# A three-stage decoder layer in float32: SyncE's transfers in program order, loads placed by hand, and the feed-forward's end moved into the next half

## The chip, the cores and the metric

The kernel runs on one core of a Trainium2 chip. The metric is the device time of one execution in microseconds (us). TensorE (PE), VectorE (DVE), ScalarE (ACT) and GpSimd (POOL) compute; SyncE (SP) issues nearly all transfers between device memory and the on-chip buffer.

## The reference, cut to what matters

Three residual stages follow one another, each behind a layer norm without learned factors. `x` has 4 batches of 1024 tokens of width 512, `ctx` 4 batches of 1024 tokens of width 384; there are 16 heads of width 32, and everything is float32.

```
def _layernorm(x, axis=-1, eps=1e-05): ...
# stage 1: gated self-attention
aperture = sigmoid(x @ Wa + ba); expression = sigmoid(x @ We + be)
inner = heads(x @ Wi); outer = heads(x @ Wo)
attn = softmax(einsum('bhqd,bhkd->bhqk', inner, outer) / sqrt(dh), -1)
attn = attn * aperture[..., :, None] * expression[..., None, :]
attn = attn / (attn.sum(-1, keepdims=True) + 1e-08)
converged = einsum('bhqk,bhkd->bhqd', attn, heads(x @ Wv))
...   # a fixed rotation and gains per head
return combined @ Wout
# stage 2: cross-attention to ctx
q = heads(query @ Wq + bq); k = heads(ctx @ Wk + bk); v = heads(ctx @ Wv + bv)
attn = softmax(clip(q k^T * scale))
return (attn v) @ Wo + bo
# stage 3: feed-forward, 512 -> 64 units, each with its own 16-wide layer
s = x @ Win + bin_
h = relu(s[..., None] * W1 + b1)            # (b, t, 64, 16)
g = einsum('btmh,mh->btm', h, W2) + b2
return g @ Wout + bout
# the layer
x = x + stage1(_layernorm(x)); x = x + stage2(_layernorm(x), ctx); x = x + stage3(_layernorm(x))
```

## The kernel before

**Units, halves, steps.** The function that runs is `moderate_path` (`general_path` is entered only if a flag, computed at the end, asks for it). Its work is a list `order` of eight units: units 0 to 3 are the self-attention of batches 0 to 3 (phase 0), units 4 to 7 the cross-attention of the same batches together with the feed-forward (phase 1). A unit has two halves of 512 query tokens, written here as 4.0 (unit 4, half 0) and 4.1. The attention of a half is 32 steps: four groups of four heads, and for each group eight tiles of 128 keys.

**A step.** It issues eight score products (L547, in the trace 16 instructions), two exps on ScalarE (L552, each 128x1024, six buffers `e`), running sums of the exps on VectorE (`es`, L558 and L560; in phase 0 also `eg`, L568), and then the `av` products of the step before (L574). Where the sums of the third and fourth head are taken by TensorE (`shared`: phase 0 and unit 7), products `sm` (L582) follow. After the last step of a group come `normalize` (copies L591, L593), one step later `add_up` (products over the partitions L604, a copy L605, then on SyncE the sums to device memory, L610 and L615, and back in another layout, `cs`, L612, L616, L620), two steps later `divide` (VectorE L628 to L643, the reciprocals to device memory, L644, and back spread over partitions, `recb`, L648), and two steps later `multiply` (VectorE L654), after which the group's quarter of `q` holds the attention's result.

**Work beside the steps.** `run(attention(u, hf), beside(u, hf))` distributes a list of items over the 32 steps of a half, by weights. The items are projections of the next unit (`pre`: `load` of weights, `x`, `ctx`, `ln` layer norm, `xT` the load of the rows just stored as blocks, `tr` their transposes on VectorE, L302, and products `k`, `q`, `v` through `columns`, L87, each evacuated by ScalarE or VectorE, L264 to L268), and the end of the half before (`post`). `post` consists of `load` (output weights `wo` and four residual tiles, L694), `o` (output projection by L87 and the addition of the residual L711), `ln` (L287 with stores of the rows, L291), `xT` (L296), `b` (the output bias, GpSimd L748), `tr`, `s` (the product with Win, L758), `h` (17 items `hidden`: a relu on ScalarE, L773, into one of two buffers `hid`, and an accumulation `g` on VectorE, L777 and L779) and `out` (two items `outputs`: products L790 into two banks, additions L796, stores L798). `weave(a, b)` spreads list `a` evenly over list `b`; `pause(n)` is an empty weight.

**Buffers.** Banks for all products of the items come from one pool of two (`bank`). Weights have three buffers (`w`, loaded at L92 or L128), residual tiles four, inputs (`inT`) two, transposed blocks (`tok`, p1) one.

**Order.** TensorE, VectorE, ScalarE and GpSimd execute in the order in which the program issues. SyncE is not in that list (L57): a scheduler puts its transfers in an order of its own. [...]

**The tail.** After the last step the remaining `add_up`, `divide` and `multiply` of the last group are issued (the list `soon`), and then the whole `post` of half 7.1, with its transposes made by TensorE (L309).

Of the kernel before, what the change touches and what calls it, by code (L numbers as in the profile page):

```python
# [16 lines left out]
P = 128  # L17
# [25 lines left out]
@with_exitstack  # L43
def decoder_kernel(ctx: ExitStack, tc: tile.TileContext, a: dict, out: bass.AP):

    nc = tc.nc
    keep = ctx.enter_context(tc.tile_pool(name="keep", bufs=1))
    flag = keep.tile([1, 1], I32, name="flag")
    E = mybir.EngineType
    with tc.manual_schedule(engines={E.PE, E.DVE, E.Activation, E.Pool}):  # L57
        moderate_path(tc, a, out, flag)
    again = nc.values_load(flag[0:1, 0:1], min_val=0, max_val=1, skip_runtime_bounds_check_because="0 or 1")
    with tc.If(again > 0):  # L60
        general_path(tc, a, out)


def moderate_path(tc: tile.TileContext, a: dict, out: bass.AP, flag: bass.AP):
    nc = tc.nc
    x = a["x"]
    with ExitStack() as st:
# [268 lines left out]
        def pre(u):  # L336
# [145 lines left out]
            def values(kt):  # L482
# [5 lines left out]
                def part(cs):  # L488
                    def f():
                        if cs[0] == 0:  # L490
                            if kt == 0:
                                me["wv"] = load_w(f"v{ph}")
                                me["v"] = p2.tile([P, NT, H, DH], F32, tag="v", name="v")
                            me["pv"] = bank()
                        for c in cs:
                            columns(
                                me["pv"], me[kind, hf, "t"](c, t), me["wv"][:, c, :],
                                start=(c == 0), stop=(c == n - 1),
                            )
                        if cs[-1] == n - 1:  # L500
                            pvh = me["pv"].rearrange("p (h d) -> p h d", d=DH)
                            if ph == 0:
                                ex = me["sw"][:, kt, :, 1].unsqueeze(2).to_broadcast([P, H, DH])
                                nc.vector.tensor_tensor(me["v"][:, kt], pvh, ex, ALU.mult)
                            else:
                                evacuate(me["v"][:, kt], pvh)
# [23 lines left out]
        def attention(u, hf):  # L530
# [5 lines left out]

            shared = ph == 0 or u + 1 == len(order)

            def scores(g, kt):
# [61 lines left out]
            def add_up(g, i, both, added):  # L601
# [11 lines left out]
                else:  # L613
# [5 lines left out]
                    for k in range(sums):  # L619
                        nc.sync.dma_start(  # L620
                            c[64:, k, :, :], s2[k].rearrange("(p h) (q e) -> (h q) p e", h=2, e=INNER)
                        )
                after(2, lambda: divide(g, i, both, c))

            def divide(g, i, both, c):
# [21 lines left out]
                for j in range(HG):  # L647
                    nc.sync.dma_start(  # L648
                        all_[j * DH : (j + 1) * DH, :], rec_d[i % 4][j : j + 1, :].to_broadcast([DH, HALF])
                    )  # L650
                after(2, lambda: multiply(g, both, all_))

# [25 lines left out]
        def post(u, hf):  # L678
# [6 lines left out]
            def load(t):  # L685
                def f():
                    if t == 0:
                        me["wo"] = load_w(f"o{ph}")
                    r = res[t] = p4.tile([P, D], F32, tag="res", name="res")
                    tt = 4 * hf + t  # L690
                    if ph == 0:
                        nc.sync.dma_start(r, x[b][tt * P : (tt + 1) * P, :])
                    else:
                        nc.sync.dma_start(r, x1b_d[b][tt])  # L694
                return f

            def project(t):
                def part(cs):
                    def f():
# [3 lines left out]
                        for c in cs:  # L703
                            columns(
                                res["po"], me["q", hf][:, c, ts(t, P)], me["wo"][:, c, :],
                                start=(c == 0), stop=(c == NC - 1),
# [79 lines left out]
            def outputs(t):  # L786
# [14 lines left out]
            loads = [[(0, load(t)) for t in range(4)]]  # L801
            r = {
                "load": loads,
                "o": [project(t) for t in range(4)],
# [44 lines left out]
        def one(f):  # L849
            return [[(0, f)]]  # L850

        def beside(u, hf):

            last = post(u, 0) if hf else post(u - 1, 1) if u else None
            if u + 1 == n:
                out = last["load"] + pause(16) + last["o"] + weave(last["ln"], pause(4)) + last["xT"] + pause(4)
                out += last["tr"] + weave(last["b"], pause(4)) + last["s"] + weave(last["h"], pause(12))
                return out + pause(2) + last["out"]
            p = pres[u + 1]
            x, ln, xT, tr, k, q, v = (p[i] for i in ("x", "ln", "xT", "tr", "k", "q", "v"))  # L860
            next_ = pres[u + 2] if u + 2 < B else None
            if u + 1 < B:
                if hf == 0:
                    if last:
                        out = x[1] + last["load"] + k[0][0:1] + p["g"][0] + k[0][1:] + p["gt"][0]
                        out += weave(ln[1], last["o"]) + xT[1] + weave(last["ln"], v[0][0:2])
                    else:
                        out = one(rotations) + one(fold_bv) + x[1] + k[0][0:1] + [rotate(c) for c in range(NC)]
                        out += p["g"][0] + k[0][1:2] + [[(4, fold_bv)]] + weave(ln[1], k[0][2:]) + p["gt"][0]
                        out += xT[1] + v[0][0:2]  # L870
                    return out + tr[1] + v[0][2:3] + p["g"][1] + v[0][3:] + p["gt"][1]
                if not next_:
                    return k[1] + last["load"] + v[1] + last["o"] + weave(last["ln"], q[0][0:2]) + q[0][2:] + q[1]
                out = next_["x"][0] + k[1][0:2] + last["load"] + weave(next_["ln"][0], k[1][2:] + v[1]) + last["o"]
                out += weave(last["ln"], q[0][0:2]) + q[0][2:] + next_["xT"][0] + q[1][0:3] + next_["tr"][0] + q[1][3:]
# [5 lines left out]
            if hf == 0:  # L881
                out = p["ctx"][0] + p["ctx"][1] + last["load"]
                if "s" not in last:
                    return out + k[0] + v[0] + last["o"] + weave(last["ln"], k[1][0:2]) + k[1][2:] + v[1][0:2]
                out += k[0][0:3] + v[0][0:1] + last["o"] + weave(last["ln"], v[0][1:3]) + last["xT"] + v[0][3:]
                out += last["b"][0:2] + k[1][0:1] + last["tr"] + k[0][3:] + last["b"][2:] + last["s"]
                return out + weave(last["h"], k[1][1:] + v[1][0:1]) + v[1][1:2] + last["out"]
            out = xT[0] + last["load"] + v[1][2:] + tr[0] + xT[1] + q[0][0:2] + last["o"][0:2] + tr[1] + last["o"][2:]
            out += weave(last["ln"], q[0][2:3])
            if "s" not in last:  # L890
                return out + q[0][3:] + q[1]
            out += last["xT"] + last["b"][0:2] + q[0][3:] + last["tr"] + q[1][0:1] + last["b"][2:] + last["s"]
# [5 lines left out]
        first += p["k"][1] + one(lambda: pres[1]["load"]("k")) + pres[1]["x"][0] + p["g"][1]  # L898
        first += weave(pres[1]["ln"][0], p["q"][1]) + pres[1]["xT"][0] + one(load_wout) + p["gt"][1]
# [668 lines left out]
```

## Time and profile before

| | us |
|---|---|
| median of 3 runs | 2324.78 |
| lowest and highest | 2324.44, 2326.49 |
| the profiled execution, its own time | 2323.08 |
| its span in the profile | 2321.1 |
| TensorE busy | 2214.6 (95%) |
| VectorE busy | 1556.0 (67%) |
| ScalarE busy | 1237.3 (53%) |
| before half 0.0 | 0 to 114.9 |
| phase 0 (0.0 to 3.1) | 114.9 to 1219.8 |
| 4.0, 4.1 | 121.8, 134.6 |
| 5.0, 5.1 | 135.0, 137.1 |
| 6.0, 6.1 | 135.1, 137.4 |
| 7.0, 7.1 to its last step | 117.0, 118.3 |
| tail | 65 |

A half is counted from its first exp (L552) to the first exp of the next. The mean granted TensorE clock is 0.982 of full speed. The share of busy time is a mean over stages that differ: a row of matmuls counts as busy also while its instructions follow one another slowly, so that lengths of halves, and of steps in them, are the better measure of where time goes. Lines of the profile name engine, line, operation, output and input; "idle before <- releaser" tells for how long the engine stood still and what ended that.

### The profile page before, as it was taken

What the parts mean: (1) busy time and instruction counts of PE and PEld (TensorE: products, weight loads), DVE (VectorE), ACT (ScalarE), POOL (GpSimd) and SP (SyncE); (2) the same over time, 40 slices, a digit from 0 to 9 for tenths busy, and PEclk for the clock granted to TensorE, in tenths of its full rate; (3) what the DMA queues carried; (4) which work ended last, traced back from release to release, by engine and by line L of the source; (5) the groups of instructions that cost most, each with busy time, mean ns of one, the idle gap of its engine ahead of it and who ended that gap; (6) DMA issues with size and microseconds to landing.
All of it is one profiled execution on the core that took longest, in us unless ns stands there. A gap on an engine that the chain in (4) does not pass through costs nothing.

```text
span 2321.1 us, 52855 instructions
## 1 busy us (share of the span) xinstructions
PE 2214.6 (95%) x22610; PEld 556.3 (24%) x22610; DVE 1556.0 (67%) x2478; ACT 1237.3 (53%) x1485; POOL 136.9 (6%) x146
## 2 busy tenths in 40 slices
PE   6999999999999999999999999998999989999984
PEld 2322222222222222222222222222222212222211
DVE  4468666786758866666775758776776757645554
ACT  0055445554455544555556555656465645657561
POOL 3000020000000000000000001010010101000000
PEclk9999999999999999999999999999999999999997
DMA  4422032041311312112222212231222332102020
GB/s 132 129 94 67 26 114 71 23 131 37 128 45 35 100 48 84 44 44 85 62 80 57 90 55 74 74 83 62 60 61 75 79 101 61 65 25 70 25 71 25
DMA packets 153862, 162.01 MB, mean 70 GB/s; under 512 B 46624, under 2 KB 92320, under 8 KB 152464
## 3 DMA queue, kind: packets, MB, share of 16 engines
q1 hardware_dynamic: 150160, 157.48, 22.6%
q8 instruction: 179, 2.93, 0.6%
q0 software_dynamic: 2144, 0.98, 0.3%
q14 instruction: 67, 0.55, 0.1%
q10 hardware_dynamic: 1312, 0.07, 0.1%
HBM read 115.68 MB, written 42.76 MB: 68 GB/s over the span
## 4 chain that ended last, share of the span: by engine, by line
PE 82%; DVE 5%; DMA 5%; ACT 4%; issue 3%; SPq 1%; DVEq 0%; ACTq 0%
PE f L87 33%; PE s L547 22%; PE av L574 18%; PE sm L582 5%; PE sm L604 3%; ACT e L552 2%; DVE es L560 2%; DMA rec_d<-rec 2%; ACT hid L773 1%; PE f L790 1%; DMA w<-in_attn_Wo 1%; DVE g L779 1%; DMA recb<-rec_d 1%; DMA rows_d<-r 1%; SPq L648 0%
## 5 line engine op out<-in xcount | busy, mean ns | idle before, releaser
L552 ACT ACTIVATE e<-s 128x1024 f32<-128x1024 f32 x1024 | 994.3, 1021 | 767.3 <-PE s L547 579.3
L560 DVE TENSOR_TENSOR es<-es,e 128x1024 f32<-128x1024 f32 x528 | 637.7, 1233 | 265.1 <-ACT e L552 263.9
L547 PE MATMUL s<-q,k 32*64 32x512 f32 x8192 | 635.0, 616 | 24.8 <-ACT e L552 22.6
L574 PE MATMUL av<-e,v 128*32 128x512 f32 x4096 | 553.7, 606 | 0.0
L87 PE MATMUL f<-xT,w 128*32 128x512 f32 x2816 | 335.7, 601 | 16.7 <-DVE xT L302 15.9
L568 DVE SCALAR_TENSOR_TENSOR eg<-e,sw,eg 128x512 f32<-128x512 f32 x448 | 318.4, 746 | 2.3
L87 PE MATMUL f<-w,q 128*32 128x512 f32 x2048 | 245.6, 597 | 11.3 <-DVE q L654 11.3
L547 PEld LDWEIGHTS s<-q,k 32*64 32x64 f32 x8192 | 138.5, 130 | 490.4 <-ACT e L552 288.3
L558 DVE TENSOR_TENSOR es<-e 128x1024 f32<-128x1024 f32 x88 | 110.3, 1276 | 205.2 <-ACT e L552 184.0
L574 PEld LDWEIGHTS av<-e,v 128*32 128x32 f32 x4096 | 88.4, 108 | 406.9 <-issue 401.4
L87 PEld LDWEIGHTS f<-xT,w 128*32 128x32 f32 x2816 | 93.2, 111 | 233.1 <-issue 205.3
L582 PE MATMUL sm<-e,sw 128*2 128x512 f32 x1024 | 133.3, 592 | 0.0
L773 ACT ACTIVATE hid<-sT,units 128x256 f32<-128x256 f32 x128 | 73.4, 600 | 72.3 <-DVE sT L268 40.7
L87 PEld LDWEIGHTS f<-w,q 128*32 128x32 f32 x2048 | 67.1, 111 | 167.5 <-issue 151.1
L719 POOL TENSOR_TENSOR r<-res,bo_bc 128x512 f32<-128x512 f32 x32 | 40.9, 1277 | 1111.5 <-DVE res L711 1056.5
L87 PE MATMUL f<-w,xT 128*32 128x512 f32 x896 | 104.6, 592 | 0.6 <-DVE q L268 0.6
L87 PE MATMUL f<-ctxT,w 128*32 128x512 f32 x768 | 92.7, 592 | 0.0
L87 PE MATMUL f<-w,ctxT 128*32 128x512 f32 x768 | 91.9, 593 | 0.0
L779 DVE SCALAR_TENSOR_TENSOR g<-hid,units,g 128x256 f32<-128x256 f32 x120 | 58.0, 483 | 34.4 <-ACT hid L773 25.2
L604 PE MATMUL sm<-es,ones 128*1 128x512 f32 x352 | 68.5, 621 | 0.7 <-ACT both L593 0.7
L654 DVE TENSOR_TENSOR q<-both,recb 128x512 f32<-128x512 f32 x64 | 45.0, 703 | 34.5 <-DMA recb<-rec_d 34.1
L287 DVE TENSOR_SCALAR r<-res,fmv,yi 128x512 f32<-128x512 f32 x60 | 37.1, 635 | 38.4 <-DMA rows_d<-r 37.8
(240 smaller groups left out, 1068.2 us busy)
## 6 DMA issues: line engine op xcount, KB each, us to landing
recb<-rec_d SPq DMA_DIRECT2D x256, 64.0 KB
xT<-rows_d SPq DMA_DIRECT2D x60, 256.0 KB
rows_d<-r SPq DMA_DIRECT2D x60, 256.0 KB
w<-in_xattn_Wo SPq DMA_DIRECT2D x9, 1024.0 KB
xin<-in_x SPq DMA_DIRECT2D x8, 1024.0 KB
res<-in_x SPq DMA_DIRECT2D x32, 256.0 KB
w<-wout_d SPq DMA_DIRECT2D x8, 1024.0 KB
x1b_d<-r SPq DMA_DIRECT2D x32, 256.0 KB
```

What stands on the lines that cost most here:

```text
L87: nc.tensor.matmul(to[r], lhsT=lhsT[:, j, :] if len(lhsT.shape) == 3 else lhsT[:, r], rhs=rhs, **flags)
L547: nc.tensor.matmul(s[m : m + 64, j, :], lhsT=k[r, g, kt * P + m : kt * P + m + 64], rhs=q[r, g, :], start=True, stop=True,)
L552: nc.scalar.activation(e, s, AF.Exp, scale=SCALE)
L558: nc.vector.tensor_tensor(me["es"][i], me["e", 0][i], es[i], ALU.add)
L560: nc.vector.tensor_tensor(me["es"][i], me["es"][i], es[i], ALU.add)
L568: nc.vector.scalar_tensor_tensor(eg, es[0][:, h, :], gate(kt), eg, ALU.mult, ALU.add)
L574: nc.tensor.matmul(av[r, :], lhsT=me["v"][:, kt, HG * g + h, :], rhs=es[h // 2][:, h % 2, :], start=(kt == 0), stop=(kt == NT - 1),)
L582: nc.tensor.matmul(sm[j * DH : j * DH + sums, :], lhsT=me["sw"][:, t, HG * g + 2 + h, :] if ph == 0 else ones, rhs=me["e", t][1][:, h, :], ...
L604: nc.tensor.matmul(sm[j * DH : j * DH + 1, :], lhsT=ones, rhs=e, start=True, stop=True)
L654: nc.vector.tensor_tensor(me["q", hf][:, g, :], both[:, 0, :], all_, ALU.mult)
L773: nc.scalar.activation(hid, res["s"], AF.Relu, bias=units[:, 1, h : h + 1], scale=units[:, 0, h : h + 1])
L779: nc.vector.scalar_tensor_tensor(res["g"], res["hid"], units[:, 2, h - 1 : h], res["g"], ALU.mult, ALU.add)
```

## The change

- **SyncE in program order.** L57 puts SyncE into the list of engines whose order is the program's. Each load of weights is an item of its own in the lists: `ahead(u, "k" | "q" | "v")` for a coming unit's, `wo` for the output weights, apart from the residual's `load`.
- **A half's feed-forward ends in the next half.** The items `h` and `out` of the half whose `s` has just been made are kept in `held`. In the next half, `end(...)` weaves the 17 hidden items with the first products (`k[0] + v[0][0:1]` in half 0, `v[1][2:] + q[0][0:2]` in half 1) and puts the outputs after them; the residual loads of the following `post` come after that.
- **Transposes earlier.** `xT[0]`, two value items and `tr[0]` go to the end of half 0; before, `xT[0]` and `tr[0]` stood at the head of half 1.
- **Unit 7.** Sums, `divide` and `multiply` are `apart` three steps instead of two. Half 7.1 makes six of the hidden items of (7, 0).
- **The tail.** The other eleven hidden items of (7, 0), the last half but one, are issued between the last group's `add_up`, `divide` and `multiply` (six and five), its `out` after them, ahead of the output projection of 7.1. The residual of 7.1 goes to a buffer of `inT`.

```
-    with tc.manual_schedule(engines={E.PE, E.DVE, E.Activation, E.Pool}):
+    with tc.manual_schedule(engines={E.PE, E.DVE, E.Activation, E.Pool, E.SP}):
...
+            apart = 2 if u + 1 < len(order) else 3
...
-                after(2, lambda: divide(g, i, both, c))
+                after(apart, lambda: divide(g, i, both, c))
...
-                after(2, lambda: multiply(g, both, all_))
+                after(apart, lambda: multiply(g, both, all_))
...
-                    if t == 0:
-                        me["wo"] = load_w(f"o{ph}")
-                    r = res[t] = p4.tile([P, D], F32, tag="res", name="res")
+                    if not last:
+                        r = res[t] = p4.tile([P, D], F32, tag="res", name="res")
+                    else:
+                        if t == 0:
+                            res["all"] = p2.tile([P, 4, D], F32, tag="inT", name="res")
+                        r = res[t] = res["all"][:, t, :]
...
+            def fetch():
+                me["wo", hf] = load_w(f"o{ph}")
...
+        held = []
+        def ahead(u, what):
+            return one(lambda: pres[u]["load"](what))
...
             last = post(u, 0) if hf else post(u - 1, 1) if u else None
+            end = lambda items: weave(held[0]["h"], items) + held.pop()["out"] if held else items
             if u + 1 == n:
-                out = last["load"] + pause(16) + last["o"] + weave(last["ln"], pause(4)) + last["xT"] + pause(4)
-                out += last["tr"] + weave(last["b"], pause(4)) + last["s"] + weave(last["h"], pause(12))
-                return out + pause(2) + last["out"]
+                out = last["wo"] + end(pause(14)) + last["load"] + pause(2) + last["o"] + weave(last["ln"], pause(8))
+                out += last["xT"] + pause(10) + last["tr"] + weave(last["b"], pause(4)) + last["s"]
+                if hf == 0:
+                    out += pause(5)
+                else:
+                    out += weave(last["h"][0:6], pause(6))
+                    last["h"] = last["h"][6:]
+                held.append(last)
+                return out
...
             if hf == 0:
-                out = p["ctx"][0] + p["ctx"][1] + last["load"]
-                if "s" not in last:
-                    return out + k[0] + v[0] + last["o"] + weave(last["ln"], k[1][0:2]) + k[1][2:] + v[1][0:2]
-                out += k[0][0:3] + v[0][0:1] + last["o"] + weave(last["ln"], v[0][1:3]) + last["xT"] + v[0][3:]
-                out += last["b"][0:2] + k[1][0:1] + last["tr"] + k[0][3:] + last["b"][2:] + last["s"]
-                return out + weave(last["h"], k[1][1:] + v[1][0:1]) + v[1][1:2] + last["out"]
-            out = xT[0] + last["load"] + v[1][2:] + tr[0] + xT[1] + q[0][0:2] + last["o"][0:2] + tr[1] + last["o"][2:]
-            out += weave(last["ln"], q[0][2:3])
-            if "s" not in last:
-                return out + q[0][3:] + q[1]
-            out += last["xT"] + last["b"][0:2] + q[0][3:] + last["tr"] + q[1][0:1] + last["b"][2:] + last["s"]
-            return out + weave(last["h"], q[1][1:]) + last["out"]
+                out = ahead(u + 1, "v") + last["wo"] + p["ctx"][1] + end(k[0] + v[0][0:1]) + last["load"] + v[0][1:2]
+                out += last["o"] + weave(last["ln"], v[0][2:])
+                if "s" in last:
+                    out += last["xT"] + weave(last["b"], k[1][0:2]) + last["tr"] + k[1][2:3] + last["s"] + k[1][3:]
+                    held.append(last)
+                else:
+                    out += k[1]
+                return out + xT[0] + v[1][0:2] + tr[0]
+            out = ahead(u + 1, "q") + last["wo"] + end(v[1][2:] + q[0][0:2]) + xT[1]
+            out += (ahead(u + 2, "k") if u + 2 < n else []) + last["load"] + q[0][2:3] + last["o"] + tr[1]
+            out += weave(last["ln"], q[0][3:] + q[1][0:1])
+            out += pres[u + 2]["ctx"][0] if u + 2 < n else []
+            if "s" in last:
+                out += last["xT"] + weave(last["b"], q[1][1:3]) + last["tr"] + q[1][3:] + last["s"]
+                held.append(last)
+                return out
+            return out + q[1][1:]
...
-        first = p["x"][0] + p["ln"][0] + p["tr"][0] + p["k"][0] + p["x"][1] + one(negate) + p["g"][0]
+        first = ahead(0, "k") + p["x"][1] + ahead(0, "q") + ahead(0, "v")
+        first += p["x"][0] + p["ln"][0] + p["tr"][0] + p["k"][0] + one(negate) + p["g"][0]
...
-        while soon:
-            soon.pop(0)[-1]()
         crossing.clear()
-        run([lambda: None], sum(post(n - 1, 1).values(), []))
+        tail, before = post(n - 1, 1), held.pop()
+        parts = lambda *names: sum((sum(tail[k], []) for k in names), [])
+        hidden = sum(before["h"], [])
+        run([lambda: None], [parts("wo", "load")])
+        soon.pop(0)[-1]()
+        run([lambda: None], [hidden[0:6]])
+        soon.pop(0)[-1]()
+        run([lambda: None], [hidden[6:]])
+        soon.pop(0)[-1]()
+        run([lambda: None], [sum(before["out"], []), parts("o", "ln", "xT", "b", "tr", "s", "h", "out")])
```

The lists of phase 0 keep their products and get `wo` and `ahead` items: in half 0 `ahead(u + 1, "v")` before the first `k` product, in half 1 `ahead(u + 1, "q")` and `ahead(u + 2, "k")` before `o`.

More of the change, by code (lines that the diff above doesn't have):

```diff
@@ L491, in f @@
                             if kt == 0:
-                                me["wv"] = load_w(f"v{ph}")
+                                if "wv" not in me:
+                                    fetch("v")
                                 me["v"] = p2.tile([P, NT, H, DH], F32, tag="v", name="v")
@@ L704, in f @@
                             columns(
-                                res["po"], me["q", hf][:, c, ts(t, P)], me["wo"][:, c, :],
+                                res["po"], me["q", hf][:, c, ts(t, P)], me["wo", hf][:, c, :],
                                 start=(c == 0), stop=(c == NC - 1),
@@ L802, in post @@
             r = {
+                "wo": [[(0, fetch)]],
                 "load": loads,
@@ L864, in beside @@
                     if last:
-                        out = x[1] + last["load"] + k[0][0:1] + p["g"][0] + k[0][1:] + p["gt"][0]
+                        out = x[1] + last["wo"] + last["load"] + ahead(u + 1, "v") + k[0][0:1] + p["g"][0] + k[0][1:] + p["gt"][0]
                         out += weave(ln[1], last["o"]) + xT[1] + weave(last["ln"], v[0][0:2])
@@ L868, in beside @@
                         out = one(rotations) + one(fold_bv) + x[1] + k[0][0:1] + [rotate(c) for c in range(NC)]
-                        out += p["g"][0] + k[0][1:2] + [[(4, fold_bv)]] + weave(ln[1], k[0][2:]) + p["gt"][0]
-                        out += xT[1] + v[0][0:2]
+                        out += ahead(u + 1, "v") + p["g"][0] + k[0][1:2] + [[(4, fold_bv)]] + weave(ln[1], k[0][2:])
+                        out += p["gt"][0] + xT[1] + v[0][0:2]
                     return out + tr[1] + v[0][2:3] + p["g"][1] + v[0][3:] + p["gt"][1]
                 if not next_:
-                    return k[1] + last["load"] + v[1] + last["o"] + weave(last["ln"], q[0][0:2]) + q[0][2:] + q[1]
-                out = next_["x"][0] + k[1][0:2] + last["load"] + weave(next_["ln"][0], k[1][2:] + v[1]) + last["o"]
+                    out = k[1] + ahead(u + 1, "q") + last["wo"] + last["load"] + v[1] + ahead(u + 2, "k") + last["o"]
+                    return out + weave(last["ln"], q[0][0:2]) + q[0][2:] + pres[u + 2]["ctx"][0] + q[1]
+                out = next_["x"][0] + k[1][0:2] + last["wo"] + last["load"] + weave(next_["ln"][0], k[1][2:] + v[1])
+                out += ahead(u + 1, "q") + ahead(u + 2, "k") + last["o"]
                 out += weave(last["ln"], q[0][0:2]) + q[0][2:] + next_["xT"][0] + q[1][0:3] + next_["tr"][0] + q[1][3:]
@@ L897, in moderate_path @@
+        first += p["x"][0] + p["ln"][0] + p["tr"][0] + p["k"][0] + one(negate) + p["g"][0]
         first += weave(p["ln"][1], p["q"][0]) + p["gt"][0] + p["xT"][1] + p["v"][0][0:3] + p["tr"][1] + p["v"][0][3:]
-        first += p["k"][1] + one(lambda: pres[1]["load"]("k")) + pres[1]["x"][0] + p["g"][1]
+        first += p["k"][1] + pres[1]["x"][0] + ahead(1, "k") + p["g"][1]
         first += weave(pres[1]["ln"][0], p["q"][1]) + pres[1]["xT"][0] + one(load_wout) + p["gt"][1]
```

## The prediction

> **What bounds the kernel now.** I read the busy times, the slices, the table by stretches (one per half), then the waits, the timelines round the longest ones, and the tail. The span is 2321.1 us.
>
> ```profile
> PE 2214.6 (95%) x22610; PEld 556.3 (24%) x22610; DVE 1556.0 (67%) x2478; ACT 1237.3 (53%) x1485; POOL 136.9 (6%) x146
> ...
> PE   6999999999999999999999999998999989999984
> ```
>
> TensorE is the bound nearly throughout, and idle for 106.5 us: by the stretches 19 before the first half, 5 in phase 0, 37 in 4.0 to 6.1 (unit 4, half 0, to unit 6, half 1), 45 in unit 7 and the tail. Since a busy matmul row includes matmuls that crawl, I measured each step from its first exp to the next step's first exp and took off its matmuls at their undisturbed durations (per instruction 0.065 us scores, 0.110 av, 0.114 L87, 0.107 sums). A step with 16 L87 instructions has 16x0.065+8x0.110+16x0.114 = 3.74 us; undisturbed ones take 3.71 to 3.76. What a step takes beyond that is its excess. Phase 0 has 0 to 4 us a half; 4.0 has 3.6, then 4.1 to 7.1 have 15.5, 12.7, 18.4, 12.6, 18.6, 21.4, 19.7. So only phase 1 and the ends have anything to win. From the stretches (length, PE busy, ...), first 4.0, then 5.1:
>
> ```profile
> 1219.80:1341.60 121.80, 121.68 (x1272) 29.92 (x1270) 80.53 (x103) 74.71 (x88) 5.12 (x4) 1.00 0.24 76
> ...
> 1611.20:1748.20 137.00, 128.18 (x1276) 30.55 (x1274) 96.24 (x130) 80.42 (x99) 6.43 (x5) 0.96 0.26 77
> ```
>
> Nearly the same number of matmuls takes 15 us more. The waits (total, times, longest) say for what:
>
> ```profile
> DVE q L654 <- DMA recb<-rec_d: 34.1, 17, 6.3
> ...
> DVE g L779 <- ACT hid L773: 25.2, 16, 2.8
> ...
> PE f L87 <- DVE xT L302: 15.9, 4, 4.9
> ...
> PE f L790 <- DVE res L796: 8.8, 3, 4.0
> ```
>
> The third is step 3 of each phase-1 half 1: the query product is issued just behind the transposes of its input. Then the clock dips too, so the step's excess is 6.64 to 6.76 against a gap of 4.92:
>
> ```profile
> 1627.12 2.48 DVE L302 STREAM_TRANSPOSE xT<-xT 128x512 f32<-128x512 f32 x4
> ...
> 1629.66 3.37 PE L87 MATMUL f<-xT,w 128*32 128x512 f32 x16 [4.92 <-DVE xT L302]
> ```
>
> The first is step 31 of 5.0 and 6.0 (excess 7.2 each). An 8 KB store of reciprocals, L644, is issued behind 1 MB of Wq and lands 9.04 us later (in the chain). VectorE stands at the multiply; an output product waits for its bank:
>
> ```profile
> 1583.55 3.02 SPq L92 DMA_DIRECT2D w<-in_xattn_Wq  x4
> ...
> 1587.96 0.34 SPq L644 DMA_DIRECT2D rec_d<-rec  x1
> ...
> 1600.64 0.69 DVE L654 TENSOR_TENSOR q<-both,recb 128x512 f32<-128x512 f32 x1 [6.34 <-DMA recb<-rec_d]
> ...
> 1606.53 2.67 PE L790 MATMUL f<-wout,g 64*128 64x512 f32 x4 [4.00 <-DVE res L796]
> ```
>
> The rest lies in the steps with hidden layers (22 to 28): ScalarE's exps wait behind `hid`, which with two buffers waits for `g` on VectorE. In the tail:
>
> ```profile
> 2258.57 0.43 SPq L694 DMA_DIRECT2D res<-x1b_d  x1
> 2259.05 0.50 SPq L610 DMA_DIRECT2D sum_d<-both  x1
> ...
> 2263.53 0.17 DVE L628 TENSOR_TENSOR both__19724<-cs 128x16 f32<-128x16 f32 x1 [9.81 <-DMA cs<-sum_d]
> ...
> 2268.99 0.69 DVE L654 TENSOR_TENSOR q<-both,recb 128x512 f32<-128x512 f32 x1 [4.79 <-DMA recb<-rec_d]
> ...
> 2269.74 13.62 PE L87 MATMUL f<-w,q 128*32 128x512 f32 x104 [11.30 <-DVE q L654]
> ```
>
> VectorE idles 9.81 and 4.79 us while the last group's sums travel, and ScalarE longer.
>
> [...] 9.04 us for 8 KB behind 1 MB, while such stores otherwise land in about 2. [...] L610 goes out 2.6 us after its data (L605 ends at 2256.5), behind residual loads. [...]
>
> **The change, part by part**, against the profiled run (2323.08). In the built program TensorE has 4313 operations instead of 4317, ScalarE 1435 instead of 1427, VectorE 3421 instead of 3408, GpSimd the same 171, SyncE 652 instead of 692. So hardly any work goes; what can move is waits.
>
> A. 4.1 loses its 17 hidden items and outputs: one set of the eight leaves the loop, since (7,0)'s goes to the tail. It loses the zone's 7.2 us, 0.9 in the output steps and eight output matmul instructions at about 0.2 (1.6): -9.7. What hides the set in the tail is in G.
>
> B. The transposes of the first query half go to the end of half 0. Behind them come two value products of 24 matmul instructions each (48x0.114 = 5.5 us) before the query product: more than the 2.49 us of four transposes. Three times 6.6, and 1.3 at 3.1 (gap 1.13): -21.2. If VectorE is behind by then, half returns (+10).
>
> C. Wq is issued at the head of half 1, and nothing of 1 MB lies close ahead of the third group's L644 at step 27 of half 0: 2x7.2 = -14.4. Cover if it stays: none, as now.
>
> D. Hidden items now run beside `k[0]` or `v[1]`, `q[0]` of the next half's first steps. Their work is the same (17 x 0.6 us ScalarE, 16 x 0.5 VectorE). The zones of 5.1 and 6.1 cost 9.5 each, of 5.0 about 5; with less beside it I let 5.1 and 6.1 come down by 2.5 each, to near 7: -5. Bounds 0 to -9.
>
> E. The four L798 stores now stand early in a half, after the hidden items, with four output matmuls for two banks that the projections also use. Behind L798 on SyncE wait residual, transpose and weight loads, and the first group's sums; their readers come 8 or more steps later. Waits at the bank: 4.0 us in the worst place now, under 1 in most. I take 2 each for 5.0 and 6.0, 1.5 each for 5.1 and 6.1, 1 each for 7.0 and 7.1: +9; bounds 0 to +14.
>
> F. Unit 7: three steps instead of two between sums, divide and multiply. Now L654 waits for its broadcast at the second group of each half, and of the small PE gaps (4.0 us in 7.0, 2.9 in 7.1) those behind it, about 1, go: -1. Six more hidden items in 7.1, in a zone that cost 8.2 for 17: +2 (bounds 0, +3). Sum +1; bounds -3 to +4.
>
> G. Tail. Residual loads no longer wait for stores ahead of L610: -2.4 of its 2.6. Eleven hidden items (about 6 us of ScalarE and VectorE) fit into 9.81+4.79 us. But the 24 L87 instructions of the first output product that now run inside the gap (2.7 us) come after it, with (7,0)'s eight output instructions, of which about 1 us is not beside other waits: +3.7. Sum +1.3. VectorE's six items before divide take 3.3 of 9.8 us and five before multiply 2.7 of 4.8, so divide and multiply are not late; if ScalarE's are, up to +6. Bounds -2 to +8.
>
> H. SyncE in program order. In 5.1 and 6.1 about 2.75 MB (transposed input, Wk, residual) precede a reciprocal store near steps 10 to 13: about 7 us late, like C, but with no bank wait behind it, so +1 each. In 1.0 and 2.0 about 4 MB stand ahead of sums: +1 each, since phase 0 lets multiplies be up to 10 us late today without a PE gap. Sum +4. No row shows this order; below, prompt sums elsewhere could give -6; above, two groups exposed at 7.2 give +15.
>
> I. At the start the same loads go in a written order: keys' weights, second input half, queries' and values' weights. The first product waits for the input's layer norm and the keys' weights either way, so 0; a wrong order costs at most one 1 MB load, about 5 us at the 210 GB/s of the stretch 100 to 115 us. The last half's residual in one other buffer: 0, since it is read only in the tail, after 9.8 us in which SyncE has nothing else of size; if late, 1 to 2.
>
> Sum: -9.7-21.2-14.4-5+9+1+1.3+4 = -35.0, so 2288.1 in the profiled run. The median of the runs shown, 2324.78, is 1.7 above it: **2289.8**.
>
> **Rivals.**
> 1. The waits only move. Hidden items in the first steps collide with projections that ScalarE and VectorE evacuate, so D is 0 and E 14, B gives back 7 and C 3.6. Sum: -9.7-14.2-10.8+14+1+1.3+4 = -14.4, so 2310. For it: the 25.2 us of `g` waiting for `hid` have one cause, two buffers, and the change leaves it. Against: 4.0, without the zone, has 3.6 us of excess, and A, B, C depend on placement alone.
> 2. Slower: SyncE's head of line. Each group's sums, reciprocals and broadcasts must pass every load that stands before them, and an L92 that waits for a weight buffer (SyncE now waits up to 20.8 us for one) holds them all. One fully exposed group costs 7.2 (step 31 of 5.0). Five of the 64 eat the gain; from six it is slower: -35+43.2 = +8.2, so 2333. For it: the scheduler's free order on SyncE goes. Against: loads are placed at heads of halves, after the buffer's last reader, and e buffers let groups of phase 0 be late by 3 to 5 us.
> 3. The change does little: the transposes' wait and the late reciprocals come back at the products behind them (B and C zero but for 5 us). -9.7-5-5+9+1+1.3+4 = -4.4, so 2320. Against: B moves the work itself ahead of an independent product.
>
> **How the numbers follow.** The forecast has 0.68, rival 1 0.17, rival 2 0.10, rival 3 0.05. The unknown terms' half widths (D 4.5, E 7, F 3.5, G 5, H 10) combine to about 14 if independent, so the main case's own range is 2276 to 2304. Extended on both sides for B, C and rival 1: 2272 to 2316; beyond it lie rival 2, rival 3 and a small part of the main case. A measurement of this kernel tells about 0.2% (4.6 us) from no change. Faster: 0.68+0.17 and a part of rival 3, 0.86; same 0.03; slower 0.11.
>
> **What would show it.** Right: no L87 wait for L302 over 1 us at step 3 of half 1; no L654 wait over 5 us in 5.0 and 6.0; 4.1 near 125 us; 5.0 to 6.1 near 128 to 132 each; L610 within 0.5 us of L605 in the tail. Wrong in E or H: PE waits on DVE L796 in the first ten steps, or L654 waits over 6 us with a PE gap behind them. Wrong as a whole: phase 0 longer than its 1105 us from 114.9 to 1219.8, which is where rival 2 would show first.

## The result and the profile after

The changed kernel takes 2274.49 us (median of four, 2271.7 to 2275.9) against 2325.64 (2324.44 to 2328.11): ratio 0.9777, 95% interval 0.976 to 0.9794. That is 51 us less; 35 were forecast. The profiled execution took 2271.7 us with a span of 2269.5, so its span is 51.6 below the one before.

The page's busy times and TensorE's slices, after:

```profile
PE 2198.3 (97%) x22610; PEld 553.9 (24%) x22610; DVE 1566.7 (69%) x2478; ACT 1237.1 (55%) x1485; POOL 148.2 (7%) x146
...
PE   6999999999999999999999999999999999999985
```

The number of matmuls is the same and TensorE idles 71 us instead of 106. The two slices that read 8 within phase 1 are gone; only the start and the tail are left. The table of stretches after, for 4.1 and then 5.1 (length, busy times of TensorE, weight loads, VectorE, ScalarE, GpSimd, granted clock, DMA share, GB/s):

```profile
1334.50:1458.30 123.80, 121.78 (x1272) 29.40 (x1272) 90.59 (x113) 73.02 (x83) 9.98 (x5) 1.00 0.28 78
...
1587.20:1715.80 128.60, 126.23 (x1280) 31.14 (x1280) 99.71 (x133) 80.17 (x99) 10.35 (x5) 1.00 0.30 84
```

5.1 is 8.5 us shorter, and its mean clock is 1.00 instead of 0.96. In 5.1 of before the granted clock is 0.50 from 1629.6 to 1631.0 and 0.59 on to 1633.0, behind the gap of 4.92 us, and 0.50 from 1714.7 to 1718.0, behind one of 3.46; what ties the two was not shown. After, both gaps are gone, and the clock is 1.00 from 1587.2 to 1620, on to 1660 and on to 1715.8. In the waits of after (total, times, longest) the query product's wait for L302 is no longer among the rows, and that for the broadcast is halved:

```profile
ACT hid L781 <- DVE g L787: 29.8, 30, 1.6
...
PE f L798 <- DVE g L787: 20.0, 4, 10.6
...
DVE q L656 <- DMA recb<-rec_d: 18.3, 7, 6.2
```

(L656 is the multiply, L646 the store of reciprocals, L650 their broadcast, L781 `hidden`, L785 the first accumulation of `g`, L787 the further ones, L798 the output product, L804 its addition.) The first row is relus that wait for a buffer. It is about what it was, for before has two such rows, one for the first accumulation and one for the others:

```profile
ACT hid L773 <- DVE g L779: 19.6, 20, 1.5
...
ACT hid L773 <- DVE g L777: 11.5, 5, 3.7
```

Nearly all of the second row is the tail's. The longest wait of the third stands in 5.1, at the group whose reciprocals go out behind 2.75 MB of rows, Wk and residual, and land 6.36 us after their issue (5.95 in 6.1, behind 2 MB of rows and residual):

```profile
1647.14 0.69 DVE L656 TENSOR_TENSOR q<-both,recb 128x512 f32<-128x512 f32 x1 [6.22 <-DMA recb<-rec_d]
```

That is step 14, and the step takes no longer than its matmuls need (excess 0.01). The seam between 5.0 and 5.1 in the timeline of after:

```profile
1576.15 0.68 DVE L656 TENSOR_TENSOR q<-both,recb 128x512 f32<-128x512 f32 x1
...
1587.64 2.48 DVE L302 STREAM_TRANSPOSE xT<-xT 128x512 f32<-128x512 f32 x4
1588.20 1.90 PE L87 MATMUL f<-w,ctxT 128*32 128x512 f32 x16
...
1592.79 1.04 PE L87 MATMUL f<-w,ctxT 128*32 128x512 f32 x8
...
1600.93 1.47 PE L87 MATMUL f<-xT,w 128*32 128x512 f32 x12
```

The multiply has no wait; the transposes end at 1590.1, and value products keep TensorE busy until the query product at 1600.9, 10.8 us later. In the tail:

```profile
2201.90 0.59 ACT L607 COPY both<-sm 128x512 f32<-128x512 f32 x1 [1.12 <-PE sm L606]
...
2202.51 0.54 SPq L612 DMA_DIRECT2D sum_d<-both  x1
...
2206.98 0.18 DVE L630 TENSOR_TENSOR both__19702<-cs 128x16 f32<-128x16 f32 x1 [1.12 <-DMA cs<-sum_d]
...
2210.45 2.08 PE L798 MATMUL f<-wout,g 64*128 64x512 f32 x4 [8.59 <-DVE g L787]
...
2212.28 0.69 DVE L656 TENSOR_TENSOR q<-both,recb 128x512 f32<-128x512 f32 x1 [1.89 <-DMA recb<-rec_d]
...
2216.49 15.67 PE L87 MATMUL f<-w,q 128*32 128x512 f32 x128 [0.18 <-DVE res L804]
```

The sums leave at once, the hidden items fill VectorE's idle 9.81 and 4.79 us (1.12 and 1.89 are left), the multiply comes 10.4 us after the copy instead of 13.1; but the output projection starts 3.5 us after the multiply, behind the outputs of (7,0). From that copy to the end it takes 67.6 us instead of 65.2.

Where the 51.6 us went, by halves (first exp to first exp), with what the prediction's terms give for each:

| stretch | predicted | measured |
|---|---|---|
| start and phase 0 | +0.7 (B -1.3, H +2) | -7.1 |
| 4.0 | 0 | 0 |
| 4.1 | -16.3 (A, B) | -10.8 |
| 5.0, 6.0 | -5.2 each (C, E) | -6.1, -6.2 |
| 5.1, 6.1 | -6.6 each (B, D, E, H) | -8.5, -8.9 |
| 7.0 | +0.4 (E, F) | -5.6 |
| 7.1 and tail | +3.9 (E, F, G) | +1.5 |

### The profile page after: what moved, and what is told of

It is laid out like the page before. It is cut to its first block, busy times and chain, and to the rows that moved or that the text cites. A ratio compares the mean times of both kernels' runs of the same rounds, so it can differ in the third digit from the quotient of the medians.

```text
span 2269.5 us, 52806 instructions
## 1 busy us (share of the span) xinstructions
PE 2198.3 (97%) x22610; PEld 553.9 (24%) x22610; DVE 1566.7 (69%) x2478; ACT 1237.1 (55%) x1485; POOL 148.2 (7%) x146
## 4 chain that ended last, share of the span: by engine, by line
PE 85%; DVE 6%; ACT 5%; DMA 2%; issue 2%; SPq 0%; DVEq 0%; ACTq 0%
PE f L87 33%; PE s L549 22%; PE av L576 19%; PE sm L584 6%; DVE es L562 4%; ACT e L554 3%; PE sm L606 3%; ACT hid L781 1%; PE f L798 1%; DMA w<-in_attn_Wo 1%; DVE g L787 1%; PE f L766 1%; DVE xT L302 0%; DMA sum_d<-both 0%; PE f L451 0%
## 5 line engine op out<-in xcount | busy, mean ns | idle before, releaser
L562 DVE TENSOR_TENSOR es<-es,e 128x1024 f32<-128x1024 f32 x528 | 648.4, 1252 | 288.6 <-ACT e L554 287.9
L781 ACT ACTIVATE hid<-sT,units 128x256 f32<-128x256 f32 x128 | 74.8, 601 | 66.2 <-DVE sT L268 36.2
L787 DVE SCALAR_TENSOR_TENSOR g<-hid,units,g 128x256 f32<-128x256 f32 x120 | 57.9, 483 | 13.3 <-ACT hid L781 4.9
L719 DVE TENSOR_TENSOR res<-f,res 128x512 f32<-128x512 f32 x64 | 43.9, 686 | 30.6 <-PE f L87 30.6
L756 POOL TENSOR_TENSOR res<-res,bout_bc 128x512 f32<-128x512 f32 x28 | 59.8, 2143 | 66.0 <-DVE r L287 65.6
```

Of the source, the lines that this page charges most:

```text
L562: nc.vector.tensor_tensor(me["es"][i], me["es"][i], es[i], ALU.add)
L756: return lambda: nc.gpsimd.tensor_tensor(res[t], res[t], bout_bc, ALU.add)
L781: nc.scalar.activation(hid, res["s"], AF.Relu, bias=units[:, 1, h : h + 1], scale=units[:, 0, h : h + 1])
L787: nc.vector.scalar_tensor_tensor(res["g"], res["hid"], units[:, 2, h - 1 : h], res["g"], ALU.mult, ALU.add)
```

## Experiments

Three theories stood against one another. **Places**: the gain comes from where the lists put transposes, hidden items and the tail. **Order**: it comes from SyncE's written order. **Buffers**: what is left, and a part of what went, is relus that wait for one of two buffers. Times are medians in us; the kernel before ran beside each, at 2324.24 (e1 to e4), 2329.38 (e5 to e8) and 2326.79 (e9 to e11). So a difference between kernels of different rounds is good to some 5 us, and where it is smaller the halves of the profiles say more.

**e1, the order to the scheduler.**

```
-    with tc.manual_schedule(engines={E.PE, E.DVE, E.Activation, E.Pool, E.SP}):
+    with tc.manual_schedule(engines={E.PE, E.DVE, E.Activation, E.Pool}):
```

> The changed kernel with SyncE's order left to the scheduler again; every list and every load stays where the change put it. If the gain comes from where the work stands (transposes, hidden items, tail), nearly all of it stays: 2270 to 2282 us, ratio to the kernel before 0.977 to 0.982. If the written order of SyncE is what gains, the scheduler will again put Wq and residual loads ahead of reciprocals: 2290 us or more, with waits of L656 for its broadcast over 6 us and matmul gaps of 4 us behind them. If a written order costs (rival 2 of the prediction, in part), it is faster than the changed kernel: under 2270.

Measured: 2309.93, ratio 0.9937 (0.9918 to 0.9956); 35 more than the changed kernel. The longer halves are 0.0 (+4.3), 2.0 (+7.8), 3.0 (+5.4), 4.0 (+5.2), 5.0 (+6.4) and 6.0 (+6.3). In the timeline of 5.0:

```profile
1560.83 2.73 SPq L92 DMA_DIRECT2D w<-in_xattn_Wq  x4
...
1565.63 0.34 SPq L646 DMA_DIRECT2D rec_d<-rec  x1
...
1574.09 1.71 SPq L650 DMA_DIRECT2D recb<-rec_d  x4
...
1575.90 3.35 SPq L291 DMA_DIRECT2D rows_d<-r  x3
...
1578.36 0.55 DVE L287 TENSOR_SCALAR r<-res,fmv,yi 128x512 f32<-128x512 f32 x1 [6.13 <-DMA rows_d<-r]
...
1587.85 2.15 PE L606 MATMUL sm<-es,ones 128*1 128x512 f32 x6 [2.73 <-DVE es L562]
```

The scheduler puts Wq at the middle of half 0, and the reciprocals go out behind it and land 8.44 us after their issue. What that costs is not a late multiply this time. The row stores L291 stand behind the broadcast on SyncE, and leave over 7 us after the first rows were ready (1568.5). The norm L287 has two buffers for its rows and waits 6.13 us until a store has left; VectorE's sums stand behind it, and TensorE's products over the partitions behind those. In 3.0, 4.0 and 6.0 the reciprocals are 8.5 to 9.1 us on their way in the same place. In 2.0 a row store itself goes out behind 1 MB of stage-1 weights, and L287 waits 7.16 us. VectorE's waits of L287 for stores are 43.2 us in all, 4.4 in the changed kernel. So these lists need the order; e9 asks whether it is the order or the loads.

**e9, the same without the early loads.** L57 as in e1, and:

```
-            return one(lambda: pres[u]["load"](what))
+            return []
```

> As e1 (the changed kernel, SyncE's order left to the scheduler), and the items that load weights ahead are taken out, so that each of Wq, Wk, Wv is issued at its first product as in the kernel before; the output weights' own item, the early transposes, the held hidden items and the tail stay. If the 36 us of e1 came from the scheduler hoisting loads that the lists issue early, it comes back to 2275 to 2285 us, with VectorE's waits of L287 for row stores far under e1's 43.2 us. If the scheduler delays stores and rows whatever the lists say, it stays near e1: 2300 to 2315.

Measured: 2285.52, ratio 0.9826 (0.981 to 0.9843): 24 of e1's 35 us are back. The profiled spans differ from the changed kernel's by 14.7, of which 5.7 lie before 0.0, and 4.6, 1.9 and 1.9 in 0.0, 0.1 and 1.0; 4.0 to 7.0 are within 0.4 each of the changed kernel. VectorE still waits 23.8 us for row stores in all. At 0.0, keys' weights for the next unit arrive late:

```profile
122.46 1.94 PE L87 MATMUL f<-xT,w 128*32 128x512 f32 x8 [4.56 <-DMA w<-in_attn_Wo]
```

So in phase 1 the scheduler's order with late loads is as good as the written one with early loads: there the written order only makes early loads harmless. At the start the two seem to pay together: half 1.0 begins at 401.0 here, at 395.5 in e1 and at 391.2 in the mean of the kernels with the written order. The written order without early loads was not run.

**e2, the transposes back in half 1.**

```
-                return out + xT[0] + v[1][0:2] + tr[0]
+                return out + v[1][0:2]
-            out = ahead(u + 1, "q") + last["wo"] + end(v[1][2:] + q[0][0:2]) + xT[1]
+            out = xT[0] + ahead(u + 1, "q") + last["wo"] + end(v[1][2:] + tr[0] + q[0][0:2]) + xT[1]
```

> The changed kernel with the first half's transposes and their load back in half 1 of phase 1, the four transposes right ahead of the query product. If the wait for L302 was worth what the step's excess said, it returns: step 2 or 3 of 3.1, 4.1, 5.1 and 6.1 grows by 5 to 6.6 us in the last three and about 1 in 3.1, sum +16 to +21, so 2291 to 2295 us. If the wait only moves (the held hidden items and the value products cover it, or the time was lost elsewhere), the sum is under +5: below 2280.

Measured: 2296.0, ratio 0.9872 (0.9838 to 0.9906): +21.5. By halves 3.1 +1.3, 4.1 +6.9, 5.1 +6.2, 6.1 +5.5, sum 19.9; the profiled spans differ by 25.5, and most of the rest lies in the start. The wait is back, in the timeline at 5.1:

```profile
1622.90 2.79 PE L87 MATMUL f<-xT,w 128*32 128x512 f32 x12 [8.85 <-DVE xT L302]
```

**e5, the transposes alone, in the kernel before.** The same two items moved, nothing else.

```
-                    return out + k[0] + v[0] + last["o"] + weave(last["ln"], k[1][0:2]) + k[1][2:] + v[1][0:2]
+                    return out + k[0] + v[0] + last["o"] + weave(last["ln"], k[1][0:2]) + k[1][2:] + xT[0] + v[1][0:2] + tr[0]
...
-                return out + weave(last["h"], k[1][1:] + v[1][0:1]) + v[1][1:2] + last["out"]
-            out = xT[0] + last["load"] + v[1][2:] + tr[0] + xT[1] + q[0][0:2] + last["o"][0:2] + tr[1] + last["o"][2:]
+                return out + xT[0] + weave(last["h"], k[1][1:] + v[1][0:1]) + v[1][1:2] + last["out"] + tr[0]
+            out = last["load"] + v[1][2:] + xT[1] + q[0][0:2] + last["o"][0:2] + tr[1] + last["o"][2:]
```

> The kernel before with one part of the change alone: in phase 1 the load of the first half's rows and the four transposes go to the end of half 0; SyncE's order stays the scheduler's. If part B stands on its own, the gaps of 4.92 us ahead of the query product in 4.1, 5.1 and 6.1 and of 1.13 in 3.1 go: -17 to -22, 2303 to 2308 us. If it needs the written order of SyncE (the scheduler puts weights ahead of the rows, as it did to reciprocals), the gap or a wait of VectorE for the rows returns: -10 at most, over 2314.

Measured: 2307.99, ratio 0.9912 (0.9893 to 0.993), 21 less than the kernel before beside it; by halves 3.1 to 6.1 lose 1.6, 5.0, 6.6 and 6.6. Part B stands on its own from both sides, and with either order of SyncE.

**e4, Wq late.**

```
-                return out + xT[0] + v[1][0:2] + tr[0]
+                return out + ahead(u + 1, "q") + xT[0] + v[1][0:2] + tr[0]
```

(and out of half 1's head)

> The changed kernel with Wq's 1 MB load moved from the head of half 1 back to the end of half 0 in phase 1 (after the last key product), so that it again stands close ahead of the third group's sums and reciprocals on SyncE, while no output product stands at the half's end. If a late reciprocal costs by itself what step 31 of 5.0 and 6.0 lost, three halves (4.0, 5.0, 6.0) lose 5 to 7 us each: +14 to +21, 2289 to 2295 us. If the loss needs the output product that waits for a bank behind the late multiply, VectorE waits 5 us or more at L656 in these halves but TensorE has no gap over 1.5: +0 to +5, under 2280.

Measured: 2287.37, ratio 0.9836 (0.9811 to 0.9861): +13. But the edit did not bring about what it was meant to test. SyncE issues Wq behind the third group's reciprocals and broadcast, not ahead of them; from the timeline of 5.0's end:

```profile
1572.63 0.34 SPq L646 DMA_DIRECT2D rec_d<-rec  x1
...
1574.05 1.72 SPq L650 DMA_DIRECT2D recb<-rec_d  x4
...
1575.87 2.51 SPq L92 DMA_DIRECT2D w<-in_xattn_Wq  x4
...
1578.48 9.38 SPq L296 DMA_DIRECT2D xT<-rows_d  x4
```

It is the same in 4.0 and 6.0, and in the changed kernel Wq goes out at nearly the same time (1575.09), but behind the rows' loads. So the edit puts Wq ahead of these loads and no more, and says nothing of late reciprocals. 4.0, 5.0 and 6.0 are unchanged at 121.8, 128.9 and 128.9; 5.1 and 6.1 get 6.1 and 7.0 longer. The rows are late behind Wq, and with them the transposes; from timelines at the heads of 4.1 and 5.1:

```profile
1345.39 2.49 DVE L302 STREAM_TRANSPOSE xT<-xT 128x512 f32<-128x512 f32 x4 [7.67 <-DMA xT<-rows_d]
...
1597.64 2.49 DVE L302 STREAM_TRANSPOSE xT<-xT 128x512 f32<-128x512 f32 x4 [7.20 <-DMA xT<-rows_d]
...
1600.46 0.60 ACT L781 ACTIVATE hid<-sT,units 128x256 f32<-128x256 f32 x1 [4.14 <-DVE g L785]
...
1606.21 2.89 PE L549 MATMUL s<-q,k 32*64 32x512 f32 x16 [5.05 <-ACT e L554]
```

VectorE stands for over 7 us in both halves. In 4.1, which has no hidden items, that costs nothing: its length is 123.8 as in the changed kernel. In 5.1 a relu waits for VectorE's `g`, the exps stand behind the relu, and TensorE waits for the exps. **Here a late VectorE cost only where another engine was tied to it.**

**e3, each half's end in its own half.**

```
-                    out += last["xT"] + weave(last["b"], k[1][0:2]) + last["tr"] + k[1][2:3] + last["s"] + k[1][3:]
-                    held.append(last)
+                    out += last["xT"] + weave(last["b"], k[1][0:1]) + last["tr"] + k[1][1:2] + last["s"]
+                    out += xT[0] + weave(last["h"], k[1][2:] + v[1][0:1]) + v[1][1:2] + last["out"]
+                    return out + tr[0]
...
-                out += last["xT"] + weave(last["b"], q[1][1:3]) + last["tr"] + q[1][3:] + last["s"]
-                held.append(last)
-                return out
+                out += last["xT"] + weave(last["b"], q[1][1:2]) + last["tr"] + q[1][2:3] + last["s"]
+                return out + weave(last["h"], q[1][3:]) + last["out"]
```

(in unit 7 likewise, and nothing held for the tail)

> The changed kernel with each half's hidden items and outputs at the end of the same half as before, and with nothing of (7,0) in the tail; SyncE's written order and the early transposes stay. If the hidden zone costs the same wherever it stands and only one of eight sets is hidden by the tail, 4.1 gets about 8 us longer, the other halves of phase 1 stay within 3, the tail gets 2 shorter: +5 to +15, 2280 to 2290 us. If moving the end into the next half is the main gain (outputs no longer at the half's end behind late reciprocals), +20 or more: over 2294.

Measured: 2302.05, ratio 0.9899 (0.9875 to 0.9924): +27.6. 4.1 is 8.4 longer as expected, but 5.0 to 6.1 are 3.9 to 5.0 longer and 7.0 2.2; 7.1 with the tail is 2.5 shorter. This is more than the prediction's A, D, E, F and G together (-3.4). The kernel overstates it, though: in half 1 of these lists the 17 items stand beside one product, in the kernel before beside three. By subtraction the held items and the tail have some 13 us of the change's 51.6: B has 19.9, step 31 of 5.0 and 6.0 has 13.4, and the start and phase 0 without B's part have 5.4. That takes the parts to add up, which was not tested.

This run also separates C from the outputs. They stand at the half's end again, but Wq does not go ahead of the third group's reciprocals, which land 1.41 us after their issue; and step 31 of 5.0 has 1.24 us of excess, against 7.23 in the kernel before.

**e7, three buffers for the relu's output.** (Room: one buffer instead of two for `gi`, and the last check's tile in `both`'s place.)

```
-                        hid = p2.tile([P, 2 * P], F32, tag="hid", name="hid")
+                        hid = p3.tile([P, 2 * P], F32, tag="hid", name="hid")
```

> The changed kernel with three buffers for the relu's output instead of two (room is made by one buffer instead of two for the gates' input in phase 0, and the last check's tile in another's place). If the 5 to 8 us of excess in the steps with hidden items come from exps that stand behind a relu waiting for its buffer, the six zones of 5.0 to 7.1 lose 2 to 4 us each: -12 to -20, 2255 to 2263 us. If they come from the work itself (17 relus and 16 accumulations beside exps and sums), or from the single chain of accumulations, within 4 of the changed kernel.

Measured: 2254.13, ratio 0.968 (0.9659 to 0.9701), 20 less than the changed kernel and the fastest of all. 5.0 to 6.1 lose 3.2, 3.8, 3.2 and 4.9, 7.0 1.8. The waits of e7:

```profile
ACT hid L781 <- DVE g L787: 6.1, 8, 1.6
```

The changed kernel's 29.8 us became 6.1. How such a wait reaches TensorE stands in the timeline of before at 5.1:

```profile
1713.14 0.60 ACT L773 ACTIVATE hid<-sT,units 128x256 f32<-128x256 f32 x1 [3.70 <-DVE g L777]
...
1713.64 1.92 ACT L552 ACTIVATE e<-s 128x1024 f32<-128x1024 f32 x2
...
1714.70 2.90 PE L547 MATMUL s<-q,k 32*64 32x512 f32 x16 [3.46 <-ACT e L552]
```

The relu waits 3.70 us for `g`, the exps behind it start 0.5 us after it does, and the score products wait 3.46 us for the first of them. With one more buffer most of these waits go.

**e11, three buffers in the kernel before.** The same edits there.

> The kernel before with three buffers for the relu's output and nothing else of the change. If the zones with hidden items in 4.1 to 7.1 lose 2 to 4 us each by it, as in e7, seven zones give -14 to -25: 2300 to 2312 us. If in the kernel before late reciprocals and the outputs at the half's end set those steps, under 8: 2317 or more.

Measured: 2300.21, ratio 0.9895 (0.9877 to 0.9913): -26.6. 4.1, 5.1 and 6.1 lose 4.8, 7.3 and 8.0, while step 31 of 5.0 keeps its excess (7.98). In these three halves the zones were mostly the buffers' doing in the kernel before too, and the late reciprocals are a thing apart. The one buffer brings the kernel before about half of what the whole change brings it.

**e10, e3 with three buffers.**

> As e3 (hidden items and outputs at the end of their own half), with three buffers for the relu's output as in e7. If the 26 us that the held items are worth in e3 come from exps behind relus that wait for a buffer, most of it goes: e3 less 20 or more, 2275 to 2283 us, within some 25 of e7 (2254). If they come from the steps at a half's end (output products for two banks, too few products left to fill steps), three buffers bring both kernels the same 20 at most, and the distance of e3 to the changed kernel (27) stays between e10 and e7 as well: near 2281. Under 2270 the buffers would be the whole of it.

Measured: 2292.93, ratio 0.9856 (0.9839 to 0.9873): only 9 less than e3, and 39 above e7. Neither expectation holds. The timeline of 4.1's end:

```profile
1437.01 2.49 DVE L302 STREAM_TRANSPOSE xn<-xn 128x512 f32<-128x512 f32 x4 [5.45 <-DMA xn<-rows_d]
...
1447.01 2.98 ACT L781 ACTIVATE hid<-sT,units 128x256 f32<-128x256 f32 x5 [2.21 <-DVE g L785]
...
1450.95 2.90 PE L549 MATMUL s<-q,k 32*64 32x512 f32 x16 [4.23 <-ACT e L554]
```

The rows come 5.45 us late for VectorE, so that the items follow with few steps left, and five relus stand in one row ahead of the exps. A third buffer does little there. What `held` gives, as far as this shows, is steps: the items wait until the next half has room. How much of e3's 27.6 is this and how much my tighter lists was not separated.

**e6, two steps in unit 7.** `apart = 2` for every unit.

> The changed kernel with two steps between sums, divide and multiply in unit 7, as before, instead of three. If that spacing made 7.0 5.6 us shorter, 7.0 and 7.1 get 3 us or more longer each: +6 or more, 2280 us. If it was worth the 1 us of the prediction, the shorter 7.0 comes from where the hidden items stand, and this kernel is within 2 of the changed one.

Measured: 2275.72, ratio 0.9775 (0.9752 to 0.9798); 7.0 takes 111.4 in both. The spacing is worth nothing there.

**e8, the outputs of (7,0) later in the tail.**

```
-        run([lambda: None], [sum(before["out"], []), parts("o", "ln", "xT", "b", "tr", "s", "h", "out")])
+        run([lambda: None], [
+            sum(tail["o"][0:1] + before["out"][0:1] + tail["o"][1:2] + before["out"][1:2] + tail["o"][2:], []),
+            parts("ln", "xT", "b", "tr", "s", "h", "out")])
```

> The changed kernel with the outputs of (7,0) in the tail behind the first and second output projection of 7.1 instead of ahead of the first. The first projection's 24 instructions that need no multiply (2.7 us) run again in the gap before it, and the projections start about 4 us earlier; against that, two waits of about 2 us for banks. If the order of these cost what term G says (+3.7), the tail is 2 to 4 us shorter: 2270 to 2273 us. If VectorE's additions set the tail's end, no change.

Measured: 2276.36, ratio 0.9769 (0.9751 to 0.9787): no gain. In the timeline of e8's tail the 24 instructions do run in the gap, and the rest starts with the multiply:

```profile
2206.45 3.12 PE L87 MATMUL f<-w,q 128*32 128x512 f32 x22
...
2218.22 1.94 PE L87 MATMUL f<-w,q 128*32 128x512 f32 x8 [8.64 <-DVE q L656]
2220.08 2.95 PE L798 MATMUL f<-wout,g 64*128 64x512 f32 x4
...
2223.01 5.82 PE L87 MATMUL f<-w,q 128*32 128x512 f32 x32
```

But the outputs then take their turns at the two banks, and the next 32 instructions start 4.8 us after the multiply's. From the last copy to the transposes L309 it is 36.0 us instead of 35.1.

## Why the prediction held, and where its steps failed

The time lies in the range, 2.5 us above its lower end, and the direction was right. The gain came out 16 us larger than the sum, so the time lies below the main case's own 2276 to 2304. The errors did not all go one way: A was 5.5 us too large, and the other terms together some 22 us too dark. Step by step:

- **B was right in kind and size.** -21.2 was predicted; 19.9 (e2, by halves) and 21 (e5) were measured, and the fear that VectorE would be behind did not come true.
- **C was right in size and in its reason:** step 31 of 5.0 went from 7.23 to 0.51, and e3 keeps most of that with the outputs back at the half's end. Where the scheduler puts Wq ahead of reciprocals again (e1), they land over 8 us after their issue and the halves lose 5.2 to 6.4. The changed kernel's third group in 5.0 has its reciprocals back 1.42 us after their issue, e3's 1.41. Why a small store lands late behind large transfers was not shown, only that it does here. What waited behind it differed: an output product for a bank in the kernel before (4.00 us), the norm for row stores in e1 (6.13), nothing that counts at step 14 of 5.1 in the changed kernel (excess 0.01). C alone was not run.
- **A was too large.** A and B gave -16.3 for 4.1; it was -10.8. The zone went, but with fewer products 4.1 now has steps that hold none (4, 12, 20 and 28, each 2.23 us long for 1.22 of matmuls, 1.01 of excess), and step 25 waits for VectorE's sums (1.93). The term forgot that a half with less beside its exps is bound by the exps in some steps: in one of these, from 1380.94 to 1383.17, the two exps take 1.94 of the 2.23 us.
- **D, E and H together were too dark in 5.0 to 6.1.** In 5.0, all but step 31 went from an excess of 5.5 to 6.5 where +2 was expected; in 5.1, from 11.8 without step 3 to 9.5 with all steps where 0 was expected. E's waits for banks hardly exist: outside the tail, output products wait 0.8 us in all for `g` (20.0 less the tail's 8.59 and 10.61) and for no bank, and +9 had been set down.
- **H was right in kind in 5.1 and 6.1**, where the reciprocals behind 2.75 and 2 MB land 6.36 and 5.95 us after their issue, but that costs nothing where +1 each was set down. 1.0 and 2.0 kept their 128.5 us to the tenth, so the loads at their heads delay nothing that counts.
- **I's zero was wrong:** start and phase 0 became 7.1 shorter, 1.7 of them B's in 3.1. Of the other 5.4, some is chance: in the eight kernels with the written start, 1.0 begins between 388.9 and 394.2 us (mean 391.2), and the profiled one is the earliest. With the start of the kernel before (three profiles, e5 and e11 among them) it begins at 394.2 to 397.7, mean 395.4. e1, which has the changed lists and the scheduler's order, begins it at 395.5. So about 4 us seem to come with the written order; which wait lies behind them stays open.
- **7.0** was to stay (+0.4) and lost 5.6. e6 excludes the spacing. Steps 22 to 28 hold the hidden items in the kernel before, steps 0 to 6 in the changed one. The count behind the excess takes the 32 instructions of the s product at 0.114 us each, though they run in about 1.9 us in all (3.11 in 7.0 of the kernel before). Counted at that, the steps with hidden items went from 12.2 to 7.9, and the same steps without them hold 4.1 and 3.9. So 4.4 of the 5.6 us lie there: the same items cost less in the first steps. Why they do was not tested.
- **G** was right but for its size: +2.4 from the last copy on, against +1.3. Sums that leave at once gave 2.7; the later projection took it back. That another order would be cheaper was wrong (e8).
- A reading was wrong, too: phase 0 was said to have 0 to 4 us of excess a half, but 0.0 has 8.9, 2.75 of it in step 10 before and after.

Of the rivals, the first was right in that relus waiting for buffers stay (31.1 us in two rows before, 29.8 after), wrong in that waits would give the gain back. The row that it names, `g` waiting for `hid`, is the other direction, VectorE early for ScalarE, and fell from 25.2 to 4.9. The second saw the right loss in the wrong kernel. In 5.0 of e1 one late group (8.44 us) held SyncE, and the row stores behind it left over 7 us after their first rows. Under the written order groups in phase 1 are that late only in 5.1 and 6.1 (6.36 and 5.95 us; the others are back in 1.41 to 2.37), at no cost, and it is the scheduler's order that loses 35 us with the same lists. The third fell with B and C, which came out whole.

## What to carry over

Measure a half by its steps against what its matmuls need, not by the busy share: in 5.1 of before the excess is 18.4 us and TensorE's idle time 8.8. It said where 7 us (transposes), 7 us (reciprocals) and 9 us (relus) of a half lay, and e5, e3 and e11 find 5 to 8 us in each of these places. Here a late VectorE cost time where relus with two buffers tied ScalarE to it (6.1 us in 5.1 of e4) and none where there were no relus (4.1). So it paid here to give such work one more buffer (20 us for 1 KB per partition, 27 in the kernel before) and to move it to where there are steps left (some 13 us, by subtraction). The loads issued early needed the written order, which in all halves of phase 1 but two keeps them behind the small stores on which others wait: in the scheduler's order the lists lose 35 us with them and 11 without.

## What the runs showed that was not expected

VectorE stood for 7.67 us (4.1 in e4) without moving the half's end by 0.1 us. Reciprocals that landed 8.44 us after their issue cost a half 6.4 us through row stores that only share SyncE with them (5.0 in e1). And the same written start ends up to 5.3 us apart between executions (388.9 to 394.2), more than several of the terms weighed here, while most halves after it repeat to 0.1 us.
